# A four-layer graph network on one core: the end of the last strip moved among layer 1's first steps

## The chip, the core and the metric

The kernel is one program on one core of a Trainium2 chip. The core has five engines that the profile names: PE (matrix products; PEld is its loading of weights), DVE, ACT and POOL (elementwise work), and SP, which here only issues transfers. Each engine works its own queue of instructions in order and waits there for what an instruction needs. Transfers (DMA) are issued from SP's or POOL's queue. SBUF is the on-chip memory of 128 partitions, PSUM the banks that PE writes its sums to, DRAM the large memory outside.

The metric is the time of one execution in microseconds (us); lower is better.

## The reference, cut to what matters

There are N = 6250 nodes with 128 features (D) and E = 206250 directed edges (100000 drawn, the same ones reversed, and one self-loop a node), sorted by destination. Each layer is `x = x + layer(h)` with `h = relu(layernorm(x))`:

```python
# layer 0: weighted sum over incoming edges
neighbor = segment_sum(edge_weight * h[src], dst)
x1 = x + leaky_relu(neighbor @ W1.T + b1 + (h * neighbor) @ W2.T + b2, 0.2)
# layer 1: mean over incoming edges (deg = count by destination), one graph
f  = gelu(segment_sum(h1[src], dst) / max(deg, 1) @ Wl.T + bl + h1 @ Wr.T)
out = f - mean_scale * mean(f)
x2 = x1 + out / sqrt(mean(out * out) + eps) * gn_weight + gn_bias + h1
# layer 2: mean of x_clique (3125 rows, later indices clamped) over outgoing edges
x3 = x2 + segment_sum(x_clique[dst], src) / max(count(src), 1) @ W.T + b
# layer 3: summed messages through a gated unit
m  = (h3 @ W_in.T + b_in) @ W_msg
x4 = x3 + gru(segment_sum(m[src], dst), h3 @ W_in.T + b_in) @ W_out.T + b_out
```

So layers 0, 1 and 3 sum over the same edges; the in-degree `deg` is a count of edges by destination.

## The kernel before, in words

The nodes form NB = 49 blocks of 128 (the last has 106 real rows). Every neighbour sum is a dense product of TensorE with a matrix of counts (or of summed weights) that the kernel first builds from the edge list. Numbers in brackets are lines of the kernel before.

**The strips.** `fast` works through NS = 25 strips of SB = 2 blocks of destinations; the last strip (k = 24) has one block. `prepare(k)` [644] fetches the strip's edges by indirect DMAs from POOL's queue and also counts the edges of each destination into `deg`, a tile of [128, 25, 2] in which each number belongs to one node (strip, partition, parity). `one_hots` [719] lets DVE build 0/1 rows. `count` [738] multiplies them on PE (line 753, PSUM tile `pK`), and ACT moves out the counts (762, tile `cnt`, 8 bits) and the summed weights (760, tile `edge_w`). A strip is 32 calls of `count`, the last one 16. When a block of destinations is complete, SP writes its counts to DRAM (`cnt_d`, line 889). `turn` [765] transposes parts of `cnt_d` for layer 2.

`layer0(k)` [782] is layer 0's product for strip k, h0 times `edge_w` (line 790), into the PSUM tile `pL` of two banks. It is a generator of 16 turns that runs during the counts of strip k+1: every second call of `count` is followed by one turn. Its result goes to `finish0` [811], a generator of seven steps that is worked off during the strip after (`END_AT`): transposes of h0, the products with W1 and W2 (824, 825), leaky relu, the sum with x, the norm, the writes of h1 (`h_d`), of x1 + h1 (`u_d`), the transposes and products with Wr (845) and the write of `f_d`. These writes go by SP's queue, for the last three strips by POOL's.

Strips 1 to 23 stand in `tc.manual_schedule()`, that is in the order in which the code emits them. The first strip and the last, and what follows the last up to layer 1 (the rest of `layer0(24)`, the ends of strips 23 and 24, the copy of `deg` to DRAM as `deg_d` [917], the check of the total count [919 to 922]), are ordered by the framework's scheduler. `edge_w` is a pool of two buffers, one for each parity of strips; layer 1's tiles are taken from the memory that the strips have given back.

**Layers 1 and 3.** `dense` [935] is written out in order by hand. It goes over 13 chunks of at most four blocks of destinations (`CHUNKS`: 4, 4, 4, 4, 4, 3, 2, then six of 4), and in each over ten steps of five (or four) source blocks. Per step, `bring` loads the counts from `cnt_d` (SP, line 961, into `ring`, one load for two steps), and DVE (973, 967) and ACT (975, 968) convert them to fp32 in `wide`; in layer 1 they also sum the counts by source (`seen`, the tile `deg2`). Then PE multiplies (line 992, tile `acc`), twice for each source block: the right-hand rows are split in an upper part (rounded) and a lower part (the rest). `bring` for the next step is emitted ahead of the products of this step.

In layer 1's first chunk the rows of h1 come in as they are needed: `h_up_to` [1038], called from `bring` on every second step, loads groups of four blocks from `h_d` (SP, 1042, three buffers) and has DVE make both parts (`halves`, 594 and 595). `inverse_degrees` [1063] reads `deg_d` back in the order of nodes, one 4-byte number at a time (1065), and takes the inverse. `load_f` [1069] brings back `f_d`.

What follows a chunk (`end1` [1115], `end2`, `end3` [1236]) is a generator; `run` and `between` advance each by one step per step of `dense`. The `chores` list [1285] hangs loads and small work on numbered steps of layer 1: `wl` and the memset of `f_sum` on step 0, `inverse_degrees` and the memset of `sq_sum` on step 1, the f loads on step 7 of chunk 0 and on step 2 of each later chunk.

Of the kernel before, what the change touches and what calls it, by code (L numbers as in the profile page):

```python
# [16 lines left out]
P = 128  # L17
# [468 lines left out]
CHUNK_OF = {g + j: (c, j) for c, (g, nb) in enumerate(CHUNKS) for j in range(nb)}  # L486
CHUNKS2 = cut(0, NB, (2, CB - 1))
# [10 lines left out]
def fast(ctx: ExitStack, tc: tile.TileContext, a: dict, out: bass.AP, flag: bass.AP):  # L498
# [10 lines left out]
    nc.vector.tensor_copy(identh, ident)  # L509
    ones = const.tile([P, P], F32, name="f_ones")  # L510
# [28 lines left out]
    u_d = dram.tile([NPAD, D], F32, name="u_d")  # L539
    f_d = dram.tile([NPAD, D], F32, name="f_d")  # L540
    h_d = dram.tile([NPAD, D], F32, name="h_d")
    x_d = dram.tile([NPAD, D], F32, name="x_d")
    smp_d = dram.tile([NSMP, 1], I32, name="smp_d")
    deg_d = dram.tile([NS, P, WN], F32, name="deg_d")
# [52 lines left out]

    with ExitStack() as bx:
# [6 lines left out]
        psum = bx.enter_context(tc.tile_pool(name="b_psum", bufs=1, space=bass.MemoryType.PSUM))  # L605
# [14 lines left out]
        deg = keep.tile([P, NS, WN], F32, name="deg")  # L620
        h0 = keep.tile([P, NB, D], F32, name="h0")
        work, edge = pool("work", 1), pool("edge", 2)
# [188 lines left out]
        def finish0(g, nb, agg):  # L811
# [23 lines left out]
            queue.dma_start(rows(h_d, g, nb), h1[:, :nb, :])  # L835
            queue.dma_start(rows(u_d, g, nb), xs[:, :nb, :])
# [12 lines left out]
            queue.dma_start(rows(f_d, g, nb), fs[:, :nb, :])  # L849
# [63 lines left out]
        for _ in chain(end, ends.pop(), turns):  # L913
            pass


        nc.sync.dma_start(deg_d.rearrange("s p w -> p s w"), deg)
# [15 lines left out]
    psum = ctx.enter_context(tc.tile_pool(name="f_psum", bufs=1, space=bass.MemoryType.PSUM))  # L933

    def dense(parts, by_node, seen=None, ahead=None):
# [42 lines left out]
        chunks = CHUNKS if by_node else CHUNKS2  # L978
        end = NB - 2 if by_node else NQB - 1
        parts_of = [q + e for q in range(0, NB, 2 * KP) for e in range(2)] if by_node else range(0, NQB, KQ)  # L980
        steps = [(c, g, nb, q) for c, (g, nb) in enumerate(chunks) for q in parts_of]
        ready = bring(*steps[0])
        yield
        for n, (c, g, nb, q) in enumerate(steps):
# [3 lines left out]
            if q == 0:  # L988
                acc = psum.tile([P, CB * P], F32, name="acc", bufs=2)
# [73 lines left out]
    def inverse_degrees():  # L1063
        with nc.allow_non_contiguous_dma(reason="one number for each node, once"):
            nc.sync.dma_start(inv1, deg_d.rearrange("s p w -> (s p w)").rearrange("(b p) -> p b", p=P))
# [42 lines left out]
    def times(agg, weight, nb):  # L1108
        pa = psum.tile([P, CB * D], F32, name="pA", bufs=2)
# [5 lines left out]
    def end1(g, nb, acc):  # L1115
# [22 lines left out]
        over_nodes(sq_sum, sq, g, nb)  # L1138

# [43 lines left out]
    def end2(g, nb, acc):  # L1183
# [7 lines left out]
        nc.sync.dma_start(xg, rows(u_d, g, nb))  # L1191
# [22 lines left out]
        nc.gpsimd.dma_start(rows(x_d, g, nb), xg)  # L1214
# [21 lines left out]
    def end3(g, nb, acc):  # L1236
# [5 lines left out]
        for i in range(2):  # L1242
            pg = psum.tile([P, CB * P], F32, name=r_z[i], bufs=2 - i)
# [19 lines left out]
        nc.sync.dma_start(x[:, :nb, :], rows(x_d, g, nb))  # L1263
# [6 lines left out]
        po = psum.tile([P, CB * D], F32, name="pA", bufs=2)  # L1270
# [12 lines left out]
    with tc.manual_schedule():  # L1283
# [104 lines left out]
```

## Time and profile before

| | |
|---|---|
| median of 9 runs | 1933.44 us (1930.83 to 1934.82) |
| the profiled execution, whole | 1938.71 us |
| its span (first to last instruction shown) | 1936.7 us |
| PE busy | 1803.0 us, 93% of the span |
| DVE, ACT, POOL busy | 1386.2, 1208.6, 451.1 us |
| line 790, layer 0's products | 622.9 us, 4900 instructions |
| line 992, layers 1 and 3 (and 2, apart) | 575.9 (and 157.5) us, 2548 (and 650) instructions |
| line 753, the counts | 406.8 us, 18816 instructions |

The profile is taken in one execution, on an engine's view each: busy time, the instructions by line, what ended each wait. The page shows the span in 40 slices of 48 us with a digit each for the busy share of every engine and for the clock that TensorE was granted (PEclk). A chain of waits leads back from the last instruction; 85% of it is PE. The strips take the first 1071 us or so, layer 1 the time up to about 1395, then layers 2 and 3. Views of the trace show the same for a stretch of time: the timeline lists instructions with their start, their duration, and in brackets the idle time before them and who ended it.

### The profile page before, as it was taken

The page shows a single profiled execution, that of the slowest core. Times are in us where ns is not written, and L with a number is a line of the kernel's source. Part 1 is how long each engine was busy: PE and PEld are TensorE (multiplying, and loading weights), DVE is VectorE, ACT ScalarE, POOL GpSimd, SP SyncE. Part 2 cuts the span into 40 slices and gives each one's busy share as a digit, 9 for nine tenths or more (in the row PEclk, how much of TensorE's full clock was granted, in tenths as well). Part 3 has the DMA queues.
Part 4 walks back from the last instruction along what each step waited for, and adds up shares of the span by engine and source line. Part 5 has one row for each costly group of instructions (what it writes and reads, how often), then busy time and mean ns, then how long its engine had stood idle before and what let it go on. Part 6 is the DMA issues. An engine that isn't in the chain of part 4 may idle for free.

```text
span 1936.7 us, 65313 instructions
## 1 busy us (share of the span) xinstructions
PE 1803.0 (93%) x28180; PEld 1521.9 (79%) x28180; DVE 1386.2 (72%) x2952; ACT 1208.6 (62%) x2834; POOL 451.1 (23%) x413
## 2 busy tenths in 40 slices
PE   0699999999999999999999699999999999999996
PEld 0678888888888888888878588988788877788774
DVE  5868888888888787887864577777687764454453
ACT  2867777777777777777763377876656654444442
POOL 3123432343333433333321011211122210000000
PEclk9799999999999999999999899999999999999998
DMA  4234545544454554544221655655455454445441
GB/s 74 78 86 95 138 106 125 114 117 117 96 131 101 120 114 110 122 95 126 70 59 49 171 172 155 184 157 154 109 159 142 133 163 127 133 113 157 130 145 45
DMA packets 299742, 232.04 MB, mean 120 GB/s; under 512 B 111184, under 2 KB 288451, under 8 KB 299443
## 3 DMA queue, kind: packets, MB, share of 16 engines
q1 hardware_dynamic: 290627, 213.46, 42.1%
q0 software_dynamic: 7952, 13.91, 2.5%
q8 instruction: 223, 3.65, 0.8%
q10 hardware_dynamic: 864, 0.39, 0.3%
q14 instruction: 76, 0.62, 0.1%
HBM read 130.53 MB, written 76.70 MB: 107 GB/s over the span
## 4 chain that ended last, share of the span: by engine, by line
PE 85%; issue 5%; DVE 4%; ACT 2%; DMA 2%; POOL 0%; SPq 0%; POOLq 0%; DVEq 0%; ACTq 0%
PE acc L992 32%; PE pL L790 29%; PE pK L753 16%; PE pA L1112 1%; PE pf L845 1%; PE po L824 1%; DMA smp_d<-in_dst 1%; PE po L825 1%; DVE agg L796 1%; ACT h L582 1%; PE pM L1228 1%; PE pB L1223 0%; DVE wide L973 0%; PE pv L708 0%; PE pA L1273 0%
## 5 line engine op out<-in xcount | busy, mean ns | idle before, releaser
L790 PE MATMUL pL<-edge_w,h 64*128 64x256 f32 (+1 forms) x4900 | 622.9, 388 | 7.0 <-issue 2.2
L992 PE MATMUL acc<-wide,parts 128*128 128x512 f32 (+2 forms) x2548 | 575.9, 384 | 11.3 <-DVE wide L973 10.5
L762 ACT CAST cnt<-pK 128x400 uint8<-128x400 f32 x784 | 394.9, 504 | 247.5 <-PE pK L753 194.9
L992 PEld LDWEIGHTS acc<-wide,parts 128*128 128x128 f32 x2548 | 462.3, 189 | 109.6 <-issue 13.4
L790 PEld LDWEIGHTS pL<-edge_w,h 64*128 64x128 f32 x4900 | 445.0, 188 | 45.4 <-DVE agg L796 6.7
L753 PEld LDWEIGHTS <-s_hot 64*128 64x128 bf16 x18816 | 381.4, 95 | 101.5 <-issue 50.3
L753 PE MATMUL pK<-k_hot,s_hot 64*128 64x49 bf16 (+1 forms) x18816 | 406.8, 193 | 47.6 <-issue 25.1
L760 ACT COPY edge_w<-pK 128x392 f32<-128x392 f32 x784 | 397.4, 507 | 0.0
L731 DVE TENSOR_TENSOR s_hot<-iota,keys 128x2048 bf16<-128x2048 bf16 x196 | 241.1, 1230 | 90.2 <-PE pK L753 77.3
L734 DVE TENSOR_TENSOR k_hot<-k_hot,by_edge 128x2352 bf16<-128x2352 bf16 x196 | 271.8, 1387 | 8.0
L973 DVE TENSOR_SCALAR_CACHE_REDUCE wide<-ring 128x512 fp32r<-128x512 uint8 (+2 forms) x325 | 193.4, 650 | 29.8 <-issue 14.6
L975 ACT ACTIVATE wide<-ring 128x512 fp32r<-128x512 uint8 (+2 forms) x312 | 184.8, 595 | 42.8 <-ACT wide L975 18.6
L641 POOL DMA_INDIRECT dst<-in_dst,off_i x50 | 82.6, 1652 | 410.7 <-DVE node L679 393.3
L968 ACT CAST wide<-ring 128x1024 fp32r<-128x1024 uint8 (+3 forms) x130 | 120.8, 957 | 71.7 <-PE acc L992 70.3
L992 PE MATMUL acc<-wide,q_parts 128*128 128x512 f32 (+2 forms) x650 | 157.5, 392 | 1.9 <-DVE wide L953 1.7
L967 DVE CAST wide<-ring 128x1536 fp32r<-128x1536 uint8 (+2 forms) x130 | 119.0, 939 | 51.9 <-PE acc L992 41.3
L992 PEld LDWEIGHTS acc<-wide,q_parts 128*128 128x128 f32 x650 | 115.6, 188 | 29.2 <-DVE wide L953 3.5
L733 DVE TENSOR_TENSOR k_hot<-iota,keys 128x800 bf16<-128x800 bf16 x196 | 112.7, 575 | 0.0
L1277 POOL DMA_DIRECT2D out<-x x12 | 10.2, 853 | 318.5 <-DVE x L1275 318.5
L641 POOL DMA_INDIRECT line<-in_dst,at_i x25 | 41.1, 1646 | 172.2 <-DVE at_i L654 169.6
L1256 DVE SCALAR_TENSOR_TENSOR wb<-pT,f_b_hh,wb 128x512 f32<-128x512 f32 (+2 forms) x13 | 9.4, 719 | 99.4 <-PE pT L1253 99.4
L641 POOL DMA_INDIRECT src<-in_src,off_i x50 | 76.3, 1526 | 15.2 <-issue 14.9
(176 smaller groups left out, 1532.1 us busy)
## 6 DMA issues: line engine op xcount, KB each, us to landing
ring<-cnt_d SPq DMA_DIRECT2D x110, 640.0 KB
cnt_d<-cnt SPq DMA_DIRECT2D x49, 800.0 KB
cntT_d<-tt SPq DMA_DIRECT2D x125, 160.0 KB
ring<-cntT_d SPq DMA_DIRECT2D x60, 320.0 KB
ring<-cnt_d SPq DMA_DIRECT2D x10, 480.0 KB
ring<-cnt_d SPq DMA_DIRECT2D x10, 320.0 KB
xs<-in_x SPq DMA_DIRECT2D x12, 256.0 KB
xs<-in_x SPq DMA_DIRECT2D x24, 128.0 KB
```

What stands on the lines that cost most here:

```text
L641: nc.gpsimd.indirect_dma_start(out=t, out_offset=None, in_=col[name], in_offset=bass.IndirectOffsetOnAxis(ap=idx, axis=0))
L731: nc.vector.tensor_tensor(s_hot, count_up(P), at(0, P), op=ALU.is_equal)
L734: nc.vector.tensor_tensor(k_hot[:, :, 1:, :NB], k_hot[:, :, :1, :NB].to_broadcast([P, tq, 3, NB, TI]), parts.to_broadcast([P, tq, 3, NB, T ...
L753: nc.tensor.matmul(pk[:, h, to], s_hot[r, u, :, t], rhs, start=j == 0, stop=True, skip_group_check=True)
L760: nc.scalar.copy(m.rearrange("p b (i h) -> p b i h", h=WN), by_block[:, 1, :NB])
L762: nc.scalar.copy(m.rearrange("p b e (i h) -> p b e i h", h=WN), by_block[:, 0].rearrange("p (b e) i h -> p b e i h", e=2))
L790: nc.tensor.matmul(pl[:, h, :w], h0[r, s, :], edge_w[r, s, :w], start=s == 0, stop=s == NB - 1)
L967: nc.vector.tensor_copy(*(v[:, :3].rearrange("p k b n -> p b k n") for v in (to, of)))
L968: nc.scalar.copy(to[:, 3:ks], of[:, 3:ks])
L973: nc.vector.tensor_scalar(to[:, k], of[:, k], 1.0, None, op0=ALU.mult, op1=ALU.add, accum_out=total)
L975: nc.scalar.activation(to[:, k], of[:, k], AF.Copy, accum_out=total)
L992: nc.tensor.matmul(acc[:, : nb * P], parts[:, s, j, :], rhs, start=s + j == 0, stop=s == end and j == 1)
```

## The change

* The last strip is written in order too. It runs `layer0(23)` and the end of strip 22 among its counts as the others do; the loop over `before` now also advances the end.
* After it, `finish0(23)` is spread over the turns of `layer0(24)` by `LAST_AT`. `layer0`'s sums lie in two PSUM tiles of one bank (`pB`, `pM`, in a pool opened at the start); those of the last strip stay there, and `last_of_0`, a generator run among layer 1's first steps, does for the last block what `finish0` did: the products, the norm, both parts of its h1 straight into `h_parts`, its row of f straight into `f`, and u_d by POOL. Its x and h0 are put aside beforehand (`last_x`, `last_h0`). The total of the check (`total`) is taken before the end of the strips.
* `deg` stays in SBUF, `deg_d` is gone: `inverse_degrees` is a generator that brings the degrees into the order of blocks by four small products with a picking matrix that POOL makes (a memset and two copies). It starts on step 3, the memsets and `wl` move to steps 2 and 3.
* The load of h1 in `h_up_to` goes by POOL's queue, and the lower part is made on POOL from the third group (block 8) on; the last block is skipped.
* `h_d`, `u_d`, `f_d` and `x_d` are laid out by partition, [128, 49, 128].
* The chunk of two blocks is the last one of layers 1 and 3 (`ORDER`).
* The buffers of `edge_w` are two pools; `pS`, `pA` and `acc` are taken from the other PSUM pool.

The core of the diff:

```diff
@@ -484,6 +484,7 @@
+ORDER = sorted(range(NCH), key=lambda c: CHUNKS[c][1] < CB - 1)
@@ -507,6 +508,9 @@
+    deg = const.tile([P, NS, WN], F32, name="f_deg")
+    deg2 = const.tile([P, NCH, NB], F32, name="f_deg2")
+    last_x, last_h0 = (const.tile([P, D], F32, name=n) for n in ("last_x", "last_h0"))
@@ -536,12 +540,11 @@
-    u_d = dram.tile([NPAD, D], F32, name="u_d")
-    f_d = dram.tile([NPAD, D], F32, name="f_d")
-    h_d = dram.tile([NPAD, D], F32, name="h_d")
-    x_d = dram.tile([NPAD, D], F32, name="x_d")
+    u_d = dram.tile([P, NB, D], F32, name="u_d")
+    f_d = dram.tile([P, NB, D], F32, name="f_d")
+    h_d = dram.tile([P, NB, D], F32, name="h_d")
+    x_d = dram.tile([P, NB, D], F32, name="x_d")
...
-    deg_d = dram.tile([NS, P, WN], F32, name="deg_d")
@@ -595,6 +598,8 @@
+    psum = ctx.enter_context(tc.tile_pool(name="f_psum", bufs=1, space=bass.MemoryType.PSUM))
@@ -617,9 +621,9 @@
-        deg = keep.tile([P, NS, WN], F32, name="deg")
...
-        work, edge = pool("work", 1), pool("edge", 2)
+        work = pool("work", 1)
+        edge = [pool(n, 1) for n in ("edge0", "edge1")]
@@ -782,18 +786,21 @@
             g, w = k * SB, nb * P
-            pl = psum.tile([P, WN, 512], F32, name="pL")
+            pl = [psum.tile([P, 512], F32, name=n) for n in ("pB", "pM")]
             for i in range(turns0):
...
                         r = slice(h * H, (h + 1) * H)
-                        nc.tensor.matmul(pl[:, h, :w], h0[r, s, :], edge_w[r, s, :w], start=s == 0,
+                        nc.tensor.matmul(pl[h][:, :w], h0[r, s, :], edge_w[r, s, :w], start=s == 0,
                                          stop=s == NB - 1)
...
                     yield
+            if k == NS - 1:
+                ends.append(pl)
+                return
             agg = work.tile([P, SW], F32, name="agg")
-            nc.scalar.copy(agg[:, :w], pl[:, 0, :w])
-            nc.vector.tensor_add(agg[:, :w], agg[:, :w], pl[:, 1, :w])
+            nc.scalar.copy(agg[:, :w], pl[0][:, :w])
+            nc.vector.tensor_add(agg[:, :w], agg[:, :w], pl[1][:, :w])
             ends.append(finish0(g, nb, agg))
@@ -859,11 +866,12 @@
+        LAST_AT = (0, 2, 4, 6, 7, 10, 13)
...
-            edge_w = edge.tile([P, NB, SW], F32, name="edge_w")
+            edge_w = edge[k % 2].tile([P, NB, SW], F32, name="edge_w")
@@ -898,28 +906,38 @@
-            for _ in chain(before, end):
+            for _ in before:
+                next(end, None)
+            for _ in end:
...
+        def total():
+            found = small.tile([P, 1], F32, name="found")
+            nc.vector.tensor_reduce(found, deg, axis=mybir.AxisListType.XY, op=ALU.add)
+            p_all = banks.tile([1, 1], F32, name="p_all", tag="pK")
+            nc.tensor.matmul(p_all, found, ones[:, :1], start=True, stop=True)
+            nc.vector.tensor_copy(flag, p_all)
...
-            for k, nb in STRIPS[1:-1]:
+            load_x(last_x[:, None, :], NB - 1, 1)
+            for k, nb in STRIPS[1:]:
...
-        strip(*STRIPS[-1])
-        end = ends.pop()
-        for _ in before:
-            next(end, None)
-        for _ in chain(end, ends.pop(), turns):
-            pass
-        nc.sync.dma_start(deg_d.rearrange("s p w -> p s w"), deg)
-        found = small.tile([P, 1], F32, name="found")
-        nc.vector.tensor_reduce(found, deg, axis=mybir.AxisListType.XY, op=ALU.add)
-        p_all = psum.tile([1, 1], F32, name="pL")
-        nc.tensor.matmul(p_all, found, ones[:, :1], start=True, stop=True)
-        nc.vector.tensor_copy(flag, p_all)
+            end = ends.pop()
+            pt = banks.tile([P, WN, 512], F32, name="pt", tag="pK")
+            for h in range(WN):
+                r = slice(h * H, (h + 1) * H)
+                nc.tensor.transpose(pt[:, h, :H], h0[r, NB - 1, :], ident[r, r])
+            nc.scalar.copy(last_h0.rearrange("p (h c) -> p h c", c=H), pt[:, :, :H])
+            total()
+            for i, _ in enumerate(before):
+                if i in LAST_AT:
+                    next(end, None)
+            for _ in chain(end, turns):
+                pass
+        last_l = ends.pop()
@@ -975,10 +992,10 @@
-        chunks = CHUNKS if by_node else CHUNKS2
+        chunks = [(c, *CHUNKS[c]) for c in ORDER] if by_node else [(c, *at) for c, at in enumerate(CHUNKS2)]
...
-        steps = [(c, g, nb, q) for c, (g, nb) in enumerate(chunks) for q in parts_of]
+        steps = [(c, g, nb, q) for c, g, nb in chunks for q in parts_of]
@@ -1038,11 +1055,14 @@
+            if g == NB - 1:
+                continue
...
-            nc.sync.dma_start(h[:, :nb, :], rows(h_d, g, nb))
-            halves(nc.vector, [h_parts[:, g : g + nb, i, :] for i in range(2)], h[:, :nb, :])
-    deg2 = late.tile([P, NCH, NB], F32, name="deg2")
+            nc.gpsimd.dma_start(h[:, :nb, :], h_d[:, g : g + nb, :])
+            hi, lo = (h_parts[:, g : g + nb, i, :] for i in range(2))
+            nc.vector.tensor_copy(hi, h[:, :nb, :])
+            (nc.gpsimd if g >= 2 * GB else nc.vector).tensor_tensor(lo, h[:, :nb, :], hi, op=ALU.subtract)
@@ -1061,13 +1081,25 @@
-        with nc.allow_non_contiguous_dma(reason="one number for each node, once"):
-            nc.sync.dma_start(inv1, deg_d.rearrange("s p w -> (s p w)").rearrange("(b p) -> p b", p=P))
-        nc.vector.tensor_scalar(inv1, inv1, 1.0, None, op0=ALU.max)
+        pick = work.tile([P, WN, SB * P], F32, name="wd")
+        nc.gpsimd.memset(pick, 0.0)
+        for h in range(WN):
+            nc.gpsimd.tensor_copy(pick[:, h, :].rearrange("p (n w) -> p n w", w=WN)[:, :, h], ident)
+        yield
+        yield
+        yield
+        p = psum2.tile([P, SB, NS], F32, name="pS")
+        for j in range(SB):
+            for h in range(WN):
+                nc.tensor.matmul(p[:, j, :], pick[:, h, j * P : (j + 1) * P], deg[:, :, h],
+                                 start=h == 0, stop=h == WN - 1)
+        nc.vector.tensor_scalar(inv1.rearrange("p (k j) -> p j k", j=SB), p, 1.0, None, op0=ALU.max)
...
-        return lambda: nc.sync.dma_start(f[:, g : g + nb, :], rows(f_d, g, nb))
+        nb = min(nb, NB - 1 - g)
+        return lambda: nc.sync.dma_start(f[:, g : g + nb, :], f_d[:, g : g + nb, :])
@@ -1136,6 +1168,37 @@
+    def last_of_0():
+        g = NB - 1
+        yield
+        agg = work.tile([P, P], F32, name="wa", bufs=5)
+        nc.scalar.copy(agg, last_l[0][:, :P])
+        nc.vector.tensor_add(agg, agg, last_l[1][:, :P])
+        inter = work.tile([P, P], F32, name="wb", bufs=3)
+        nc.vector.tensor_mul(inter, agg, last_h0)
+        yield
+        po = psum2.tile([P, D], F32, name="pT")
+        nc.tensor.matmul(po, agg, w1, start=True, stop=False)
+        nc.tensor.matmul(po, inter, w2, start=False, stop=True)
+        full = work.tile([P, D], F32, name="wc")
+        nc.vector.tensor_add(full, po, b12)
+        nc.vector.scalar_tensor_tensor(full, full, 0.2, full, op0=ALU.mult, op1=ALU.max)
+        nc.vector.tensor_add(last_x, last_x, full)
+        h1 = work.tile([P, 1, D], F32, name="wd")
+        yield from norm(last_x[:, None, :], h1, 1)
+        halves(nc.vector, [h_parts[:, g, i, :] for i in range(2)], h1[:, 0, :])
+        nc.gpsimd.tensor_tensor(last_x, last_x, h1[:, 0, :], op=ALU.add)
+        nc.gpsimd.dma_start(u_d[:, g, :], last_x)
+        yield
+        pt = psum2.tile([P, P], F32, name="pT")
+        nc.tensor.transpose(pt, h1[:, 0, :], ident)
+        ht = work.tile([P, P], F32, name="wc")
+        nc.scalar.copy(ht, pt)
+        yield
+        pf = psum2.tile([P, D], F32, name="pT")
+        nc.tensor.matmul(pf, ht, wr, start=True, stop=True)
+        nc.vector.tensor_add(f[:, g, :], pf, bl)
@@ -1284,10 +1347,10 @@
-        chores[0] += [load(wl, "WlT"), lambda: nc.gpsimd.memset(f_sum, 0.0)]
-        chores[1] += [inverse_degrees, lambda: nc.gpsimd.memset(sq_sum, 0.0)]
-        for c, (g, nb) in enumerate(CHUNKS):
-            chores[c * n1 + (7 if c == 0 else 2)].append(load_f(g, nb))
+        chores[2] += [load(wl, "WlT"), lambda: nc.gpsimd.memset(f_sum, 0.0)]
+        chores[3] += [lambda: running.append(inverse_degrees()), lambda: nc.gpsimd.memset(sq_sum, 0.0)]
+        for i, c in enumerate(ORDER):
+            chores[i * n1 + (7 if i == 0 else 2)].append(load_f(*CHUNKS[c]))
@@ -1301,6 +1364,7 @@
+        running.append(last_of_0())
```

More of the change, by code (lines that the diff above doesn't have):

```diff
@@ L602, in fast @@
         keep = pool("keep", 1)
-        psum = bx.enter_context(tc.tile_pool(name="b_psum", bufs=1, space=bass.MemoryType.PSUM))
         banks = bx.enter_context(tc.tile_pool(name="b_banks", bufs=3, space=bass.MemoryType.PSUM))
@@ L834, in finish0 @@
             nc.gpsimd.tensor_tensor(xs[:, :nb, :], xs[:, :nb, :], h1[:, :nb, :], op=ALU.add)
-            queue.dma_start(rows(h_d, g, nb), h1[:, :nb, :])
-            queue.dma_start(rows(u_d, g, nb), xs[:, :nb, :])
+            queue.dma_start(h_d[:, g : g + nb, :], h1[:, :nb, :])
+            queue.dma_start(u_d[:, g : g + nb, :], xs[:, :nb, :])
             yield
@@ L848, in finish0 @@
                                  bcast(bl, nb))
-            queue.dma_start(rows(f_d, g, nb), fs[:, :nb, :])
+            queue.dma_start(f_d[:, g : g + nb, :], fs[:, :nb, :])
         for by_edge in prepare(0):
@@ L932, in fast @@
     psum2 = ctx.enter_context(tc.tile_pool(name="f_psum2", bufs=1, space=bass.MemoryType.PSUM))
-    psum = ctx.enter_context(tc.tile_pool(name="f_psum", bufs=1, space=bass.MemoryType.PSUM))
     def dense(parts, by_node, seen=None, ahead=None):
@@ L988, in dense @@
             if q == 0:
-                acc = psum.tile([P, CB * P], F32, name="acc", bufs=2)
+                acc = psum2.tile([P, CB * P], F32, name="acc", bufs=2)
             for s, rhs in now:
@@ L1108, in times @@
     def times(agg, weight, nb):
-        pa = psum.tile([P, CB * D], F32, name="pA", bufs=2)
+        pa = psum2.tile([P, CB * D], F32, name="pA", bufs=2)
         for j in range(nb):
@@ L1190, in end2 @@
         xg, fg = x[:, :nb, :], f[:, g : g + nb, :]
-        nc.sync.dma_start(xg, rows(u_d, g, nb))
+        nc.sync.dma_start(xg, u_d[:, g : g + nb, :])
         nc.gpsimd.tensor_tensor(xg, xg, bcast(b_res, nb), op=ALU.add)
@@ L1213, in end2 @@
         nc.gpsimd.tensor_tensor(xg, xg, bcast(b_out, nb), op=ALU.add)
-        nc.gpsimd.dma_start(rows(x_d, g, nb), xg)
+        nc.gpsimd.dma_start(x_d[:, g : g + nb, :], xg)
         yield
@@ L1242, in end3 @@
         for i in range(2):
-            pg = psum.tile([P, CB * P], F32, name=r_z[i], bufs=2 - i)
+            pg = (psum2, psum)[i].tile([P, CB * P], F32, name=r_z[i], bufs=2 - i)
             s = slice(i * D, (i + 1) * D)
@@ L1262, in end3 @@
         x = work.tile([P, CB, D], F32, name="x", bufs=3)
-        nc.sync.dma_start(x[:, :nb, :], rows(x_d, g, nb))
+        nc.sync.dma_start(x[:, :nb, :], x_d[:, g : g + nb, :])
         yield
@@ L1269, in end3 @@
         yield
-        po = psum.tile([P, CB * D], F32, name="pA", bufs=2)
+        po = psum2.tile([P, CB * D], F32, name="pA", bufs=2)
         for j in range(nb):
```

## The prediction

> **What bounds the kernel now.** I read the page first, slice by slice. TensorE (PE) is busy at 9 tenths or more in nearly every 48 us slice, so only places where PE idles or runs at a low clock can give time: the start, the seam between the strips and layer 1 (slice 23), and the end.
>
> ```profile
> PE   0699999999999999999999699999999999999996
> PEclk9799999999999999999999899999999999999998
> ```
>
> Next I read busy time by windows around the seam. The columns are window, its length, then busy us and (instructions) of PE, PEld, DVE, ACT, POOL, then granted clock, DMA share, GB/s.
>
> ```profile
> 1005.00:1010.00 5.00, 2.11 (x42) 1.46 (x40) 0.29 (x1) 1.54 (x4) 0.00 (x0) 0.93 0.08 4
> 1010.00:1015.00 5.00, 4.27 (x68) 3.73 (x70) 3.09 (x3) 1.95 (x5) 0.00 (x0) 0.50 0.00 0
> 1070.00:1080.00 10.00, 3.40 (x34) 2.38 (x30) 2.84 (x12) 1.23 (x4) 2.05 (x4) 0.71 0.28 87
> 1080.00:1090.00 10.00, 6.45 (x20) 4.88 (x20) 5.23 (x15) 3.18 (x10) 0.99 (x2) 0.78 0.66 84
> 1090.00:1100.00 10.00, 6.08 (x18) 4.88 (x19) 7.42 (x18) 5.98 (x19) 0.00 (x0) 0.66 0.73 226
> 1100.00:1110.00 10.00, 9.99 (x43) 7.41 (x42) 9.83 (x30) 3.86 (x13) 0.00 (x0) 1.00 0.90 283
> ```
>
> There are two holes, one at 1005 and one at 1070 to 1100; behind 1100 DVE is full. The timeline tells what stands in them (start, us, engine, line, then idle time before and who ended it).
>
> ```profile
> 972.68 0.35 SPq L889 DMA_DIRECT2D cnt_d<-cnt  x1
> 992.15 0.36 SPq L889 DMA_DIRECT2D cnt_d<-cnt  x1
> 1000.75 0.36 SPq L917 DMA_DIRECT2D deg_d<-deg  x1
> 1019.69 0.35 SPq L889 DMA_DIRECT2D cnt_d<-cnt  x1
> 1043.60 0.36 SPq L889 DMA_DIRECT2D cnt_d<-cnt  x1
> ...
> 1009.40 0.24 PE L753 MATMUL pK<-k_hot,s_hot 64*128 64x49 bf16 x3 [2.11 <-issue]
> ...
> 1080.18 0.69 DVE L973 TENSOR_SCALAR_CACHE_REDUCE wide<-ring 128x512 fp32r<-128x512 uint8 x1 [2.44 <-DMA f_d<-fs]
> 1080.97 0.41 SPq L1065 DMA_DIRECT2D inv<-deg_d  x1
> 1093.92 16.52 PE L992 MATMUL acc<-wide,parts 128*128 128x512 f32 x60 [6.50 <-DVE wide L973]
> ```
>
> L889 marks the end of each block of 128 destinations. Steps are 19.5 and 20.5 us in turn (40.0 a strip); the last two are 27.5 and 23.9, so 7.0 and 4.4 us are lost. Layer 1 then waits for the last block's f_d write (its tiles lie under layer 1's), and again behind the 4-byte pieces of inv<-deg_d.
>
> **The change, part by part.** Sums are against the profiled execution: span 1936.7 us, 1938.71 in all, 5.3 above the median of the nine runs, 1933.44. I carry the difference over to the median.
>
> 1. *deg_d goes.* Its write, 3200 pieces of 8 bytes, starts at 1000.75. In the trace's DMA packets it runs until 1007.4; a 16 KB fetch of the instruction queue then takes 3.85 us, where every other takes 1.85 or less, and PE waits for "issue" (2.11 and 1.08) and restarts at clock 0.50. Nothing else is new in that strip, so I take all 7.0 off; bounds 0 and 7.0.
>
> 2. *The last strip in written order.* The scheduler's order loses 4.4 us in the last block: PE waits 1.87 for an evacuation that ACT holds behind h (which waits 1.81 for f_shift), and 0.95 for agg. Every strip in written order holds its step, so −4.4; bounds 0 and −4.4.
>
> 3. *The tail of finish0 for strips 22 and 23.* Two small products and transposes now stand inside layer 0's products for strip 23 and no longer in a wait: +1.0. So these products, which ended at 1054.8, end at 1044.4. Layer 0 for the last block took 16.1 from there (1070.9). It needs the same products, but DVE now has five conversions of 0.605 us for layer 1 ahead of strip 23's closing arithmetic: +0.5. End: 1061.0.
>
> 4. *The seam.* ring and wide now lie where strip 23's weights were, and those are free by 1044.4. So the first 20 products of layer 1 (two steps) are ready at 1061.0. last_of_0 adds some 1.8 us of PE, 3.2 of DVE (its rows in the tail: 0.29, 0.15 to 0.22 each) and 0.7 of ACT; beside the wait named next all this is covered.
>
> 5. *The loads of h and the lower parts on POOL.* This is the term that decides. h_up_to emits, for each group of four blocks: load on POOL, upper part on DVE, lower part on POOL. POOL's queue goes in that order, so a load is not issued before the lower part of the group before it is done, which waits for its own load. Before, SP ran the loads up to three ahead. DVE is relieved of ten subtractions of 0.69, but it holds the conversions of a step behind the upper parts: it too waits for each load. One round is a load (L, from issue to the consumer's start), 0.50 on DVE (row 0.43) and 1.35 on POOL:
>
> ```profile
> L595 POOL TENSOR_TENSOR q_parts<-h,q_parts 128x512 fp32r<-128x512 f32 x6 | 7.8, 1292 | 0.5
> ...
> 1491.04 0.48 SPq L1191 DMA_DIRECT2D x<-u_d  x1
> 1494.61 1.31 POOL L1192 TENSOR_TENSOR x<-x,f_b_res 128x512 f32<-128x512 f32 x1 [1.75 <-DMA x<-u_d]
> 1038.00 0.76 POOL L836 DMA_DIRECT2D u_d<-xs  x1
> 1040.40 0.17 DVE L556 MEMSET xs<- 32x128 f32 x1 [5.65 <-DMA u_d<-xs]
> ```
>
> No row has a 256 KB load from POOL. From above: the same bytes loaded by SP, in 512-byte pieces and behind a ring load, took 3.6 us here and 4.0 at most. From below: 128 KB written from POOL, 2.4. The new layout makes 2 KB pieces, and in the starved stage the rings are loaded ahead. I take **L = 3.0**, between them and off the upper end by the ring's share; both ends stay for the range.
>
> The rounds: the lower part of blocks 12 to 15 stands behind the last block's agg and inter, 2.85 after 1061.0, at 1063.85. Then follow eight loads (blocks 16 to 44), the last ending with DVE's part: 8L + 8 × 0.50 + 7 × 1.35 = 8L + 13.45. In POOL's order between them: two memsets 1.05, memset and two copies of inverse_degrees 1.1, last_x's sum and u_d write with their wait 1.3; and once DVE waits for the products of f and inv1, which stand behind a step on PE, 1.2. Together 8L + 18.1. PE then has its last two steps: first conversion 0.65, 18 products at 0.227 = 4.1, and 2.0 because PE restarts at a low clock (x20 took 6.45 us at 0.78 in the window of 1080). Chunk 0 ends at 1063.85 + 8L + 18.1 + 6.75 = 1088.7 + 8L = 1112.7 with L = 3.0. Before, its accumulator was copied out at 1115.6, so it ended at 1115.5: **−2.8**. Had only PE counted, it would end at 1085.
>
> 6. *The two-block chunk last.* It is the last of layers 1 and 3. The end of layer 3:
>
> ```profile
> 1914.54 0.58 ACT L1105 COPY wa<-acc 128x512 f32<-128x512 f32 x1 [5.68 <-PE acc L992]
> 1924.46 2.04 PE L1273 MATMUL pA<-f_W_outT,wd 128*128 128x128 f32 x8 [3.87 <-DVE wd L1268]
> 1927.52 0.74 POOL L1280 DMA_DIRECT2D out<-x  x1 [19.76 <-DVE x L1275]
> ```
>
> From copy to write 13.0 us at 512 columns. At 256 the rows of the small chunk give: copy 0.37, five products of 0.43, DVE 0.48 and 0.42, ACT 0.51, three of 0.42, four products, 0.42, with the waits 7.4. But the closing products of a four-block chunk (6 × 0.86 + 0.89 = 6.05) now stand before the accumulator's end and those of two blocks (3.0) behind it: +3.0. Together **−2.6**; bounds −1 and −4. In layer 1 PE has no idle time at its end worth naming.
>
> 7. *At nothing:* h_d, u_d, f_d, x_d by partition (issues of 0.36 on SP and 1.29 on POOL grow shorter under a PE that is full; cover gone, some 0.1 us each), last_x's load, the sums in two PSUM tiles, the reordered f loads.
>
> Sum: −2.8 − 2.6 = −5.4, so 1938.7 becomes 1933.3, and by the median **1928.0 us**.
>
> **Rules weighed.** The Trainium skill, "DMA: Bandwidth & Descriptors", section "Anatomy of one DMA — SWDGE (gpsimd) path", puts a POOL-issued transfer at about 2.0 us plus its bytes over 436 KB a us: an estimate from it is 2.6 us for 256 KB, and the sum would be −8.6. "SBUF — State Buffer", section "SBUF: two separate sides", speaks against the change: while DVE copies fp32 in its two-port mode GpSimd can't write descriptors, so loads from POOL are held up; no run here shows that for these loads, and at one upper part (0.43) per load the sum would be −2.0.
>
> **Rivals.**
> *Slower: the rounds grow.* Each us of L costs 8. The whole sum is zero at L = 3.0 + 5.4/8 = 3.7, and SP's own load took 3.6 to 4.0. For it: descriptors made on POOL, HBM reads beside ring and f loads. Against: few transfers in that stage. At L = 4.4 it gives +5.8: 1939.
> *No gain in strip 23:* the pause at 1007 is of the instruction stream and returns. +7.0 on the forecast: 1935. Against: it is the only fetch of that length.
> *The rounds overlap:* the change then does what its words promise, and chunk 0 is paced by PE (some 1085): −30.4 − 2.6, 1900. For it: DVE and PE have the room. Against: POOL's order, as far as it can be read from the code.
>
> **Numbers.** Forecast 0.55, slower 0.22, no gain in strip 23 0.15, overlap 0.08. About 0.2% (3.9 us) is what a measurement can tell from no change. Forecast: faster 0.43, same 0.12; slower rival: 0.18 slower, 0.04 same; strip 23: 0.11 same, 0.03 slower, 0.01 faster; overlap: faster 0.08. Together 0.52, 0.27, 0.21. Low end: L = 2.4 (−4.8), a tail of −4 and 4 us of steps 2 and 5 better than taken: 1918. High end: L = 4.4, 1939. The overlap and longer loads stay outside.
>
> **What would show it.** Right: L889's last steps 20.5 and 19.5; no fetch near 4 us; in chunk 0 POOL alternating load, wait, lower part at 4.9 us a round, PE idle some 5 to 10 us before the third, fifth, seventh and ninth step, its clock below 1; first acc copy near 1112.7; tail near 7.4. Wrong: PE full from layer 1's first step on (overlap), or rounds over 5.6 us (slower).

## The result, and the profile after

The changed kernel takes **1941.84 us** (median of 10 runs, 1939.68 to 1943.97), the kernel before 1933.66 (30 runs, the nine among them): a ratio of 1.0041, 95% interval 1.0032 to 1.0050, so 6 to 10 us slower. The forecast was 1928.0, its range 1918 to 1939. The profiled execution took 1941.28 us, its span is 1939.5.

The same two rows of the profile's page, after the change:

```profile
PE   0699999999999999999999599999999999999997
PEclk9699999999999999999999799999999999999998
```

The hole in slice 23 is still there and a little deeper. Windows around the seam (window, length, busy us and instructions of PE, PEld, DVE, ACT, POOL, then clock, DMA share, GB/s):

```profile
1005.00:1010.00 5.00, 5.00 (x128) 4.22 (x127) 3.42 (x4) 3.99 (x10) 0.00 (x0) 1.00 0.01 3
1070.00:1080.00 10.00, 6.50 (x20) 4.70 (x20) 4.87 (x17) 3.38 (x11) 4.50 (x6) 0.83 0.49 154
1080.00:1090.00 10.00, 4.08 (x10) 3.24 (x11) 4.65 (x16) 1.72 (x5) 5.58 (x9) 0.57 0.10 29
1090.00:1100.00 10.00, 3.81 (x14) 2.83 (x13) 1.80 (x5) 3.33 (x11) 2.62 (x3) 0.84 0.38 122
1100.00:1110.00 10.00, 8.28 (x30) 6.51 (x29) 3.32 (x12) 2.67 (x8) 2.70 (x4) 0.74 0.43 126
1110.00:1120.00 10.00, 7.72 (x27) 6.26 (x28) 8.30 (x26) 1.84 (x6) 1.26 (x1) 0.83 0.28 86
```

The hole at 1005 is gone. The other now reaches from 1065 to 1112, and in it no engine is full: PE, DVE, POOL and the transfers all idle by turns, the mark of a chain through several queues. POOL's timeline shows the chain (start, us, engine, line, idle time before and who ended it):

```profile
1062.08 1.29 POOL L1064 TENSOR_TENSOR parts<-h,parts 128x512 fp32r<-128x512 f32 x1 [1.84 <-DVE parts L1063]
1063.31 0.56 POOL L1061 DMA_DIRECT2D h<-h_d  x1
1070.09 1.27 POOL L1064 TENSOR_TENSOR parts<-h,parts 128x512 fp32r<-128x512 f32 x1 [6.22 <-DVE parts L1063]
...
1076.93 0.56 POOL L1061 DMA_DIRECT2D h<-h_d  x1
1080.60 1.25 POOL L1064 TENSOR_TENSOR parts<-h,parts 128x512 fp32r<-128x512 f32 x1 [3.11 <-DVE parts L1063]
1081.81 0.56 POOL L1061 DMA_DIRECT2D h<-h_d  x1
1085.36 1.26 POOL L1064 TENSOR_TENSOR parts<-h,parts 128x512 fp32r<-128x512 f32 x1 [2.99 <-DVE parts L1063]
...
1089.38 0.54 POOL L1061 DMA_DIRECT2D h<-h_d  x1
1094.47 1.26 POOL L1064 TENSOR_TENSOR parts<-h,parts 128x512 fp32r<-128x512 f32 x1 [4.56 <-DVE parts L1063]
```

Load, wait, lower part, load: the rounds that step 5 foretold, 4.7 to 4.9 us each where nothing else is on the way, and longer for the loads at 1063 and 1089. PE's products of line 1009, in the same stretch:

```profile
1060.62 4.83 PE L1009 MATMUL acc<-wide,parts 128*128 128x512 f32 x20
1070.65 6.50 PE L1009 MATMUL acc<-wide,parts 128*128 128x512 f32 x20 [4.76 <-DVE wide L990]
1085.92 7.50 PE L1009 MATMUL acc<-wide,parts 128*128 128x512 f32 x20 [8.77 <-DVE wide L990]
1099.71 4.63 PE L1009 MATMUL acc<-wide,parts 128*128 128x512 f32 x10 [6.19 <-DVE wide L990]
1105.71 2.58 PE L1009 MATMUL acc<-wide,parts 128*128 128x512 f32 x10
1112.28 10.38 PE L1009 MATMUL acc<-wide,parts 128*128 128x512 f32 x38 [3.99 <-DVE wide L990]
```

It waits before the third, fifth, seventh and ninth step, as said. The conversions named as releaser are not late by themselves: they stand in DVE's queue behind an upper part (line 1063) that waits for its load:

```profile
1084.84 0.43 DVE L1063 CAST parts<-h 128x512 fp32r<-128x512 f32 x1 [4.33 <-DMA h<-h_d]
1085.18 0.68 DVE L990 TENSOR_SCALAR_CACHE_REDUCE wide<-ring 128x512 fp32r<-128x512 uint8 x1
```

At the other end of the program, SP's queue and PE:

```profile
1902.84 0.37 SPq L978 DMA_DIRECT2D ring<-cnt_d  x1
1916.21 0.28 SPq L1344 DMA_DIRECT2D out<-x  x1
1916.59 0.37 SPq L978 DMA_DIRECT2D ring<-cnt_d  x1
```

```profile
1915.21 2.95 PE L1009 MATMUL acc<-wide,parts 128*128 128x256 f32 x20
1921.00 3.92 PE L1009 MATMUL acc<-wide,parts 128*128 128x256 f32 x18 [2.84 <-DVE wide L984]
```

Line 1344 writes the last 106 rows of the output. In the kernel before it was SP's last instruction. With the two-block chunk last it belongs to the chunk before, waits for that chunk's x, and behind it stands the load of the last counts, for which PE waits.

The stages, from SP's writes of counts and ACT's copies of the accumulators in the timelines (us; the second to fourth profile of before and the second of after are from the experiments below, partly on other chips):

| | before, 1st | before, 2nd to 4th | after, 1st | after, 2nd |
|---|---|---|---|---|
| step of block 47 (holds the degrees' write before) | 27.5 | 23.3, 23.3, 24.6 | 20.3 | 20.2 |
| step of block 48 | 23.9 | 23.0, 23.9, 23.9 | 19.5 | 19.5 |
| from there to chunk 0's copy | 72.0 | 71.3, 71.7, 71.6 | 86.3 | 86.8 |
| to layer 3's first copy | 478.0 | 479.3, 478.0, 478.2 | 477.9 | 479.1 |
| to layer 3's last copy | 320.9 | 320.9, 320.9, 320.9 | 328.9 | 329.0 |
| to the end of the span | 22.2 | 20.3, 20.7, 21.5 | 14.5 | 14.4 |

### The profile page after: what moved, and what is told of

Same layout as the page of the kernel before. It is cut to its first block, busy times and chain, and to the rows that moved or that the text cites. A ratio compares the mean times of both kernels' runs of the same rounds, so it can differ in the third digit from the quotient of the medians.

```text
span 1939.5 us, 65342 instructions
## 1 busy us (share of the span) xinstructions
PE 1805.9 (93%) x28187; PEld 1534.0 (79%) x28187; DVE 1380.3 (71%) x2942; ACT 1208.9 (62%) x2835; POOL 463.7 (24%) x436
## 5 line engine op out<-in xcount | busy, mean ns | idle before, releaser
L794 PE MATMUL pB<-edge_w,h 64*128 64x256 f32 (+1 forms) x2450 | 614.9, 386 | 1.4 <-ACT edge_w L764 1.0
L794 PE MATMUL pM<-edge_w,h 64*128 64x256 f32 (+1 forms) x2450 | 615.3, 386 | 0.0
L1009 PE MATMUL acc<-wide,parts 128*128 128x512 f32 (+2 forms) x2548 | 582.8, 387 | 27.8 <-DVE wide L990 24.3
L1009 PEld LDWEIGHTS acc<-wide,parts 128*128 128x128 f32 x2548 | 467.3, 191 | 127.7 <-DVE wide L990 27.1
L757 PEld LDWEIGHTS <-s_hot 64*128 64x128 bf16 x18816 | 387.7, 95 | 95.6 <-issue 49.6
L757 PE MATMUL pK<-k_hot,s_hot 64*128 64x49 bf16 (+1 forms) x18816 | 414.1, 192 | 41.8 <-issue 23.0
L794 PEld LDWEIGHTS pB<-edge_w,h 64*128 64x128 f32 x2450 | 423.1, 187 | 29.4 <-ACT edge_w L764 1.1
L794 PEld LDWEIGHTS pM<-edge_w,h 64*128 64x128 f32 x2450 | 423.0, 187 | 1.0 <-issue 0.4
```

The source lines that it names most:

```text
L757: nc.tensor.matmul(pk[:, h, to], s_hot[r, u, :, t], rhs, start=j == 0, stop=True, skip_group_check=True)
L794: nc.tensor.matmul(pl[h][:, :w], h0[r, s, :], edge_w[r, s, :w], start=s == 0, stop=s == NB - 1)
L1009: nc.tensor.matmul(acc[:, : nb * P], parts[:, s, j, :], rhs, start=s + j == 0, stop=s == end and j == 1)
```

## The experiments

Chips differ (below), so each kernel is compared by its ratio to the kernel before on the same chip. Theory 1 is that a load of h1 stands behind the lower part before it in POOL's queue, so that the rounds cannot overlap.

**The loads three groups ahead.** Same loads, same engine for the lower parts, other order in POOL's queue:

```diff
-    to_split = list(GROUPS)
+    to_split, to_load, loaded = list(GROUPS), [t for t in GROUPS if t[0] < NB - 1], []
...
-            h = whole.tile([P, GB, D], F32, name="h")
-            nc.gpsimd.dma_start(h[:, :nb, :], h_d[:, g : g + nb, :])
+            while to_load and len(loaded) < 3:
+                h = whole.tile([P, GB, D], F32, name="h")
+                nc.gpsimd.dma_start(h[:, : to_load[0][1], :], h_d[:, to_load[0][0] : sum(to_load[0]), :])
+                loaded.append(h)
+                to_load.pop(0)
+            h = loaded.pop(0)
             hi, lo = (h_parts[:, g : g + nb, i, :] for i in range(2))
```

> The changed kernel, with the loads of h1 issued up to three groups ahead (in POOL's queue they stand before the lower parts of the groups before them). Same loads, same engine for the lower parts. Theory 1 (rounds: a load is not issued before the lower part before it): chunk 0 is then paced by DVE and PE and ends 23 to 30 us earlier, 1088 to 1095 where it was 1118; time 1912 to 1919. Theory 2 (POOL's lower parts of 1.28 us set the pace): no gain beyond 3 us. Theory 3 (loads from POOL get slow beside the loads of counts, 4.6 and 6.3 us where the others took 2.9 to 3.2): loads of 4.5 to 6 us each when they overlap, gain under 10 us.

Measured: 1872.76 us where before took 1891.31, ratio 0.9907 (0.9894 to 0.9921). Chunk 0 is copied 59.0 us after the last counts' write where it was 86.3. POOL's timeline:

```profile
1031.24 0.55 POOL L1062 DMA_DIRECT2D h<-h_d  x1 [0.30 <-POOL parts L1068]
1031.81 1.27 POOL L1068 TENSOR_TENSOR parts<-h,parts 128x512 fp32r<-128x512 f32 x1
1033.38 0.68 POOL L1062 DMA_DIRECT2D h<-h_d  x1 [0.30 <-POOL parts L1068]
1034.09 1.28 POOL L1068 TENSOR_TENSOR parts<-h,parts 128x512 fp32r<-128x512 f32 x1
```

Two lower parts within 2.3 us, no wait for a load between them. Theory 1 holds; POOL's 1.28 us and slow loads do not set the pace.

**SP for the loads; DVE for the lower parts; and the changed kernel again**, on one chip.

```diff
-            nc.gpsimd.dma_start(h[:, :nb, :], h_d[:, g : g + nb, :])
+            nc.sync.dma_start(h[:, :nb, :], h_d[:, g : g + nb, :])
```
```diff
-            (nc.gpsimd if g >= 2 * GB else nc.vector).tensor_tensor(lo, h[:, :nb, :], hi, op=ALU.subtract)
+            nc.vector.tensor_tensor(lo, h[:, :nb, :], hi, op=ALU.subtract)
```

> The changed kernel, unchanged, beside the three below on one chip, as their measure. Theory 1 expects chunk 0 of layer 1 to end 86 us after the write of the last block's counts again (86.3 in the first profile), with loads of h1 of 2.9 to 3.2 us when alone and 4.6 to 6.3 beside loads of counts; ratio to before 1.004.

> The changed kernel with the loads of h1 issued by SP as before; the lower parts stay on POOL. Theory 1 (the pair costs: a load behind the lower part before it in one queue): SP does not wait for POOL's work, so the loads run up to three groups ahead and chunk 0 ends some 59 to 62 us after the last counts' write where it was 86; about 25 us less than the changed kernel, ratio to before 0.990 to 0.992. Rival (loads in SP's queue stand behind loads of counts that wait for their buffers, and so come as late): less than 12 us gained.

> The changed kernel with all lower parts on DVE as before; the loads of h1 stay on POOL. Theory 1: POOL's queue then holds loads only, which run up to three ahead; DVE has ten more subtractions of 0.69, so chunk 0 ends 62 to 68 us after the last counts' write; about 20 us less than the changed kernel. Rival (loads from POOL are slow as such, 2.9 to 6.3 us one after the other): less than 8 us gained.

Measured, beside 1930.41 for before: the changed kernel 1939.48 (1.0046; 1.0030 to 1.0061), chunk 0 after 86.8 us; loads on SP 1910.53 (0.9901; 0.9887 to 0.9915), after 57.1 (59 to 62 were expected); lower parts on DVE 1920.83 (0.9950; 0.9936 to 0.9963), after 66.6. Either edit alone breaks the rounds: what costs most is the pair in one queue, a load behind a lower part. With the lower parts on DVE chunk 0 still ends 9.5 us later than with the loads on SP. With SP's loads PE is nearly full in the seam:

```profile
1060.00:1070.00 10.00, 9.35 (x42) 6.94 (x40) 8.04 (x25) 4.58 (x16) 5.88 (x6) 1.00 0.50 159
1070.00:1080.00 10.00, 8.85 (x40) 6.35 (x40) 7.69 (x25) 5.28 (x18) 6.33 (x9) 1.00 0.87 278
1080.00:1090.00 10.00, 9.92 (x44) 7.61 (x44) 9.16 (x30) 6.33 (x20) 2.65 (x2) 1.00 0.66 216
```

With the lower parts on DVE one thing on POOL still holds up loads, the sum of last_x for the last block:

```profile
1065.34 0.53 POOL L1088 COPY wd<-f_ident 128x128 f32<-128x128 f32 x2
1075.68 0.46 POOL L1191 TENSOR_TENSOR last_x<-last_x,wd 128x128 f32<-128x128 f32 x1 [9.81 <-ACT wd L585]
1076.43 0.56 POOL L1192 DMA_DIRECT2D u_d<-last_x  x1 [0.29 <-POOL last_x L1191]
1076.99 1.59 POOL L1061 DMA_DIRECT2D h<-h_d  x3
```

**Why two loads are longer.** Fewer loads of counts during the rounds:

```diff
-    ring = ctx.enter_context(tc.tile_pool(name="f_ring", bufs=3))
+    ring = ctx.enter_context(tc.tile_pool(name="f_ring", bufs=4))
...
-        chores[2] += [load(wl, "WlT"), lambda: nc.gpsimd.memset(f_sum, 0.0)]
+        chores[2] += [lambda: nc.gpsimd.memset(f_sum, 0.0)]
+        chores[9].append(load(wl, "WlT"))
```

(The load of mean_scale moves to step 9 as well, and the copies of the accumulator have four buffers for five.)

> The changed kernel with four buffers for the loads of counts (one buffer less for the copies of the accumulator) and the loads of wl and mean_scale on step 9, so that fewer loads of counts are issued during chunk 0's rounds. Theory (a load of h1 waits in the transfer engines behind the packets of a load of counts issued before it): the load of blocks 16 to 19, 6.3 us from issue to use, falls to 4.5 or less, that of blocks 32 to 35, 4.6, to 2.9; chunk 0 ends 82 to 84 us after the last counts' write where it was 86.3 and 86.8. Rival (the two loads are late for something on POOL's own queue): no change in either.

Measured: 1944.06 (1.0047; 1.0029 to 1.0066), chunk 0 after 85.2 us. The first long load fell to 4.8 us, the second took 5.0: missed. A load of counts still ran beside each, and the loads of wl and mean_scale, though moved to step 9, were still issued at 1064.5 and 1064.1, just ahead of the first long load (1064.9). SP's issues around the first long load (1063.31) in the changed kernel:

```profile
1062.32 0.54 SPq L978 DMA_DIRECT2D ring<-cnt_d  x1
1062.90 0.62 SPq L1081 DMA_DIRECT2D f_mean_scale<-in_mean_scale  x1
1063.87 0.56 SPq L978 DMA_DIRECT2D ring<-cnt_d  x1
```

The trace's DMA packets show the same with and without the edit: a load alone has its first packet 1.25 to 1.38 us after the issue and lasts 1.2 to 1.5; beside a load of counts on SP's queue (changed kernel, SP's packets 1062.9 to 1071.5 and 1090.2 to 1092.9) the first packet comes after 3.3 and 2.9 us, with the edit after 2.6 and 2.9. For the second long load it starts, in three profiles (1092.27, 1088.94 and, with the edit, 1092.26), within 0.01 us of the first of the 16 packets of 4 bytes that end the load of counts. That the loads wait in the transfer engines behind a load of counts is the likeliest reading; no edit that frees them shows it. The other rule weighed in the prediction, that DVE's copies hold up POOL's descriptors, does not explain these two: DVE stood idle for 7.58 and 4.83 us until they landed, and the load at 1072.2, beside a busy DVE, took 2.9.

The Trainium skill, "DMA: Bandwidth & Descriptors", section "Queues, rings and completion order", has each transfer engine take turns between queues packet by packet, a packet being typically 9 to 17 descriptors and at most 64. The trace has 512 rows for a load of counts, 32 for each of 16 engines, in some 2.7 us; the waits beyond a load alone, 2.0 and 1.6 us, are then some 24 and 19 rows (an estimate). If a row is one descriptor, that is above the typical packet and under the ceiling, so the rule is neither shown nor refuted here. The page's estimate for a load alone, 2.6 us (the section named in the prediction), agrees with the trace up to the last packet, 2.5 to 2.8 us after the issue; DVE starts 0.3 to 0.4 us later, 2.9 to 3.2 after it.

**The last rows on POOL.**

```diff
-            nc.sync.dma_start(out[(NB - 1) * P :, :], x[:NR, nb - 1, :])
+            nc.gpsimd.dma_start(out[(NB - 1) * P :, :], x[:NR, nb - 1, :])
```

> The changed kernel, with the write of the last 106 output rows issued by POOL and not by SP. Theory: this write, now of the last but one chunk, stands in SP's queue ahead of the load of the last counts and waits for that chunk's x, so PE waits 2.8 us for its last conversions and then runs 1.3 us slower: 3 to 4 us faster, 1938.3, last accumulator copied out about 1921. Rival: the longer last chunk (23.3 us against 16.8) is the closing products of the four-block chunk and nothing else: under 1 us.

Measured: 1894.93 (1.0021; 1.0012 to 1.0030) against 1.0041 and 1.0046 without the edit, on other chips: some 4 us, as expected. Layer 3 from its first copy takes 324.4 where it took 328.9; the last load of counts is issued by 1867, and PE runs through (its timeline with this edit):

```profile
1872.20 1.13 PE L1336 MATMUL pA<-f_W_outT,wd 128*128 128x128 f32 x8
1873.08 5.11 PE L1009 MATMUL acc<-wide,parts 128*128 128x256 f32 x38
```

**The order of chunks alone**, in the kernel before (`ORDER` in `dense` and in the f loads), without and with that edit:

> The kernel before with one part of the change: the chunk of two blocks is the last of layers 1 and 3. The prediction took this as 2.6 us faster. Theory now: the write of the last 106 rows stands in SP's queue ahead of the load of the last counts, which costs some 4 us: last chunk 23.2 us (16.8 without the four-block closing products and the wait), end of it 7.7 instead of 13.0, so between no change and 2 us slower by the whole time, ratio 1.000 to 1.001. Rival (the order gains as predicted): 0.9987, 2.6 us faster.

> The kernel before with the two-block chunk last and the last rows written by POOL. Theory: the wait of 2.8 us in the last chunk is gone, which then takes 18.7 us (as in the changed kernel with the same edit): 4 us less than the one beside it, ratio to before 0.9975 to 0.9985.

Measured on one chip: 1937.55 (1.0014; 1.0004 to 1.0023) and 1935.61 (1.0006; 0.9997 to 1.0015). The stage shows the 4.3 us (layer 3 from 328.7 to 324.4), the total only 2: from the last copy to the end of the span it took 17.3 in place of 15.7. The first agrees with what was expected; the second missed it (0.9975 to 0.9985). So no gain from the order can be measured in this kernel even with the rows out of the way. What moves the end of the program stays open.

**The degrees.** The kernel before with `deg` kept in SBUF and the four small products, and the kernel before itself under the profile:

```diff
-        nc.sync.dma_start(deg_d.rearrange("s p w -> p s w"), deg)
...
-        chores[1] += [inverse_degrees, lambda: nc.gpsimd.memset(sq_sum, 0.0)]
+        chores[1] += [lambda: running.append(inverse_degrees()), lambda: nc.gpsimd.memset(sq_sum, 0.0)]
```

> The kernel before with one part of the change: the degrees stay in SBUF and are put in order by four small products; no write of 8-byte pieces and no read of 4-byte pieces. If the write's pieces cause the pause at 1007 us in every execution and the 4-byte reads hold up chunk 0 (waits of PE of 3.6 and 6.5 us): 7 + 5 = 12 us faster by the median. If the pause is an accident of one profiled execution: only the reads' part, about 5 us faster.

> The kernel before, unchanged, for a second profiled execution. Why: by the profiles the change costs 2.6 us (1938.7 to 1941.3), by the medians 8.2 (1933.7 to 1941.8). Theory A: the first profile of before was itself slow by some 5 us, at the pause of the instruction stream at 1007 us (7.0 us over the usual 20.5); then this profile reads about 1933.5 and the step of the last full strip's first block is 20.5, not 27.5. Theory B: the pause belongs to every execution (the 8-byte pieces of the degrees' write cause it); then it is here again, 27.5 us, and the difference lies elsewhere.

> The kernel before, unchanged, once more under the profile. The four executions of kernels with the degrees' write lost 3.9, 5.2, 5.7 and 7.0 us in the block where that write runs. If the first profile's 7.0 is the upper end of that spread, this one lies below it, and an execution's total follows it. If the 5.3 us between the first profile and the median of the runs lie elsewhere, another stage is shorter here than in the first profile by 2 us or more.

> As the one above, a third profile of the kernel before: the same two expectations.

Measured: without the degrees' write 1885.45 against 1891.31 (0.9967; 0.9955 to 0.9979), 5.9 us. SP's timeline of the kernel before (second profile), then of the edit:

```profile
949.74 0.36 SPq L889 DMA_DIRECT2D cnt_d<-cnt  x1
...
957.43 0.79 SPq L917 DMA_DIRECT2D deg_d<-deg  x1
...
973.05 0.35 SPq L889 DMA_DIRECT2D cnt_d<-cnt  x1
```

```profile
948.90 0.36 SPq L888 DMA_DIRECT2D cnt_d<-cnt  x1
...
968.34 0.35 SPq L888 DMA_DIRECT2D cnt_d<-cnt  x1
```

The step of 23.3 falls to 19.4. All six executions of kernels with this write have one 16 KB fetch of the instruction queue of 3.2 to 4.1 us in that block; in the ten executions without it no 16 KB fetch lasts over 2.0. So the pause is in every execution, but it costs 4.0, 4.0, 5.3, 5.4, 5.7 or 7.2 us (against the step without it on a chip of that speed, 19.3 or 20.3), and the first profile had the longest. (The block is the second of its strip, not the first as the expectation has it.) Neither expectation holds whole: it is no accident, and no fixed 7 us. The reads' part was taken as 5 us; from the last counts' write to chunk 0's copy the edit takes 69.8 where the kernel before took 71.3 to 72.0, so it is nearer 2. The second to fourth profiled executions took 1889.74, 1894.72 and 1895.33 us, on chips where before takes 1891.31 and 1894.11 (the latter one run). Behind the strips no stage of the last two is shorter than in the first profile by 2 us; the end comes nearest (20.7 and 21.5 against 22.2).

**Both edits together**, loads ahead on POOL or on SP:

> The changed kernel with the loads of h1 issued three groups ahead on POOL and with the last output rows written by POOL. The two gains lie in different stages and should add: 25 to 27 us in chunk 0 and 3 to 4 us at the end, ratio to before 0.988 to 0.990; faster than both kernels. Rival (one slack is used up by the other): no more than the loads alone gave, 0.991.

> The changed kernel with the loads of h1 issued by SP and the last rows written by POOL: the best version these experiments point to. 0.9901 for the loads and 4 us of 1930 for the rows: ratio to before 0.988, about 27 us less than the changed kernel. Rival (the loads ahead on POOL are as good): within 2 us of 0.9881.

Measured: 1907.92 beside 1930.41 (0.9881; 0.9866 to 0.9896) and 1910.22 beside 1934.40 (0.9875; 0.9858 to 0.9893). The gains add, and both versions beat both kernels by over 20 us.

## Why the prediction was wrong

By its own base, the first profile, the sum was −5.4 and came out at +2.6; by the medians at +8.2. In the profile the differences add up: chunk 0's copy +2.5, from there to layer 3's first copy −0.1, on to the last write +2.8, behind it −2.4, so +2.8 of the span. Two terms failed: L, the length of a load, was taken too short, and the step on the order of chunks left out an instruction. Point by point:

*Step 1, the degrees' write, −7.0:* right in this profile (27.5 to 20.3), and the mechanism is shown. But 7.0 is the top of what the six executions show; 4.0 to 5.7 is the usual.

*Step 2, the written order, −4.4:* right: 23.9 became 19.5.

*Steps 3 and 4:* right. Strip 23's sums were copied at 1044.1 (said: ended 1044.4), the first products of layer 1 began at 1060.6 (said: 1061.0). The block's end ran under the waits.

*Step 5, the rounds, chunk 0's end at 1112.7:* mechanism and place right, **size wrong**: 1118.1. L was taken as 3.0. The loads took 6.3, 2.9, 3.2, 3.0, 4.6, 2.9, some 2.9 and 2.9 from issue to DVE's start, 28.7 in all, a mean of 3.6: +4.7. The sentence that failed is that in the starved stage the rings are loaded ahead: two loads of counts were issued at 1062.3 and 1063.9, around the load at 1063.3, and another at 1088.7, just ahead of the one at 1089.4. The upper end, "4.0 at most", was also too low: in the packets of the kernel before, the load that SP issued at 1087.3 behind a load of counts ended at 1092.4 at the earliest, 5.0 us. DVE took up the seventh load 3.3 us later than its 2.9 us would allow, because it waited for the products of f and the inverse degrees, where 1.2 was taken (+2.1). The rounds began 0.5 earlier, POOL's own work in them was 0.6 shorter and the last two steps 0.3: together +5.4. The slower rival named this mechanism and put the whole sum's zero at L = 3.7; the measured 3.6 used up nearly all of the gain.

*Step 6, the two-block chunk last, −2.6:* **wrong in sign**. From layer 3's first copy to the last write the kernel takes 2.8 us more (333.9 to 336.7). From copy to write it is 7.7, as foretold (7.4). But the step from the chunk before is 23.3, not 16.8 + 3.0: the write of the last rows was not counted as an instruction that the chunk carries along in SP's queue, past a load of counts. Taking it out gave back 4.6: the step is then 18.7, and the stretch from first copy to last write 331.8 to 331.9 in four profiles, 1.1 to 2.1 below the 333.0 to 333.9 of the kernel before. So the sum of this step was sound but for that term. Unforeseen, the program's end behind the last write is shorter by 2.4 (9.2 to 6.8 us).

*The carry to the median:* wrong by 5.6 us. The first profile of before had the longest pause (2.3 above the mean of the other five) and the longest end (1.4 above the mean of its other three profiles). The rest, some 2, was not found: 0.6 of it is that the changed kernel's profile lies below its own median, and ahead of the last strips the executions on chips of that speed differ by more than the remainder (block 45's counts were written at 969.6 to 973.9).

*The overlap rival, 1900, chance 0.08:* it did not happen, but the room was there: with the loads ahead or on SP chunk 0 ends 27 to 30 us earlier, at best 57.1 us after the last counts' write, which is 1089 in the first profile's time, where 1085 was the bound. The best version has 24 of the 33 us.

## What to carry to other kernels

Issuing a load from a queue that also computes on what was loaded turns a prefetch into a chain: ask what stands between two loads on their queue, and either emit the loads ahead or leave them to a queue that does not compute. When an order of tiles is changed, list every instruction that the tile carries along on every queue, its last store too, and what stands behind it. And when a sum is worked out against one profiled execution, stages that vary between executions should be bounded by their spread.

## What the runs showed of the hardware

* With a write in 3200 pieces of 8 bytes, a 16 KB fetch of instructions took 3.2 to 4.1 us in all six executions, 2.0 at most in the ten without it; PE had single waits of 1.1 to 3.1 us there.
* The same kernel took 1891 to 1895 us on two chips and 1930 to 1934 on the others. The difference lies in the strips: on the first two a strip of two blocks took 38.4 to 38.5 us, on the others 39.9 to 40.1, while layer 1 behind its first chunk took 263.4 to 263.7 on both. In the counts' products PE's weight loads (line 753) waited 21.6 us for "issue" on one chip (second profile) and 50.3 on another (first profile).
